# Six of sixteen units by ScalarE and TensorE, a new order of the units, and softplus right behind the silu

## The chip, the cores and the metric

The kernel runs on one core of one Trainium2 chip. Time is device time in microseconds (us) of one execution; the kernel before has a median of 26257.85 us over three runs (26257.84 to 26273.53).

## The reference, cut to what matters

Layer 0 is a two-dimensional Mamba block on x of shape (8, 64, 128, 128), along rows and along columns, forwards and backwards; layer 1 is a residual block of two 3x3 convolutions with batch norms. Nearly all of the time is in layer 0:

```python
def selective_scan(u, delta, A, Bm, Cm, D):
    def step(h, inp):
        u_t, d_t, B_t, C_t = inp
        dA = jnp.exp(d_t[..., None] * A)
        h = dA * h + (d_t * u_t)[..., None] * B_t[:, None, :]
        y = jnp.einsum('bdn,bn->bd', h, C_t)
        return (h, y)
    ...
    return jnp.transpose(ys, (1, 0, 2)) + u * D

def mamba(seq, p):                       # seq: sequences of 128 steps, 64 channels
    xz = jnp.einsum('blc,ec->ble', seq, in_w)
    x, z = (xz[..., :di], xz[..., di:])  # di = 128
    x = silu(causal_conv(x, conv_w, conv_b))
    xdbl = jnp.einsum('bld,ed->ble', x, xp_w)
    dt, Bm, Cm = ...                     # 4, 16 and 16 of xdbl
    delta = jax.nn.softplus(jnp.einsum('blr,dr->bld', dt, dt_w) + dt_b)
    A = -jnp.exp(A_log)                  # (128, 16)
    y = selective_scan(x, delta, A, Bm, Cm, Dp)
    y = y * silu(z)
    return jnp.einsum('bld,cd->blc', y, out_w)
```

The results of both directions and both orientations are averaged, group-normalized, passed through a silu and added to x.

## The kernel before, in words

**Groups.** The first stage, some 25,100 of the 26,239 us, is a loop over 512 groups: 8 images, 2 orientations (`o` 0 rows, 1 columns), 32 groups of four sequences each (N = 512 time steps side by side). A group computes both directions d. Its preparation (`prepare`) runs interleaved with the scans of the group before it.

**Units.** A group's state has 128 channels x 16 states x 2 directions. It is cut into 16 units: half (0 or 1: 64 channels), `ng` (four of the 16 states), d. A unit's tile is 128 partitions (32 channels x 4 states) by 1024 (two blocks of channels x 512 steps). `ORDER` (line 34) gives for each place r of 0 to 15 its (ng, d) and its kind; half is r % 2. Of every unit a scan is made on VectorE (`scan`, lines 453 and 455): s = dA * s + (delta u B). Then GpSimd multiplies it with C (`weigh`, line 460), and TensorE adds the states up in PSUM (`add_up`, line 476).

**Where the scan's two operands come from** depends on the kind:
- The decay exp(delta A) is a pair of ScalarE activations (`decay`, line 421) on the replicated `dl`. For V and G it goes to PSUM (`dA0`, `dA1`, one buffer per half, so that of unit r + 2 can only be written when scan r is done); for T into the unit's own tile `s` in SBUF, some steps early (`EARLY`).
- delta u B is for V a VectorE product of the replicated `du` with B rows that TensorE makes in PSUM (`drive` and `b_rows`, lines 430 and 410); for G the same product on GpSimd with B loaded by DMA (`b_tile`, line 403); for T sixteen ScalarE activations per ng (`spread`, line 372: X = duT times a column of BT) which both halves share, and eight TensorE transposes per unit (`turn`, line 439) into that half's PSUM buffer.

**The round trip.** `delta` and `delta u` come out of `prepare` with channels on partitions and have to be replicated over the four states. They are stored to DRAM (`keep`: `dd`, line 314, eight stores) and loaded back with each row repeated four times (`replicate`: `dl` and `du`, line 381, 512 KB each, four of each per group, five buffers each). B and C go the same way (`bd`, line 330, from `bc`, which ScalarE copies out of PSUM at line 328; `c` at line 395, 256 KB each, eight per group). All of these DMAs are issued by SP in the order of the program; an issue whose buffer is not free holds up those behind it.

**Order.** The order of instructions on every engine is written out by hand: under `tc.manual_schedule()` the loop at the end of the first stage goes through steps s, and in step r = s % 16 it emits, in this sequence: `b_rows` (table `ROWS`), `turn` or `decay` of unit r + 1, early decays (`EARLY`), the V drive of unit r + 1, G drives ahead of time (`AHEAD`), scan and weigh of unit r, the gate of the group before at r = 3 (`gate`, line 483), one piece of the next group's `prepare`, spreads (`SPREAD`), `add_up` four steps behind, and fetches of `c` and `bt` (`FETCH`). Every engine works its own list strictly in that order and waits where an operand or a buffer is not there.

`prepare` is a generator; each `yield` ends a step's piece. Before: step 1 z (`zp`), step 2 its copy to SBUF (line 285) and the convolution `cp` (line 290), step 5 silu of u (line 297) and of the z of the group before (line 299), step 6 the matmul `dp` (line 304), step 8 softplus (line 307), step 9 `bp`, the product delta u on VectorE (`du`, line 326), `bc`, `bd`, the decay of unit 11, `dl`, its two edge copies from `far` (line 336) and the stores. Steps 10 to 15 hold the replicating loads, transposes of `du` for T units, and BT (line 362).

Softplus, silu and exp need different activation tables on ScalarE; each change is an instruction ACT_TABLE_LOAD. Beside the groups run, for part of the time, the group norm of the image before (one silu and one addition per group) and its first convolution (one tile per group).

Of the kernel before, what the change touches and what calls it, by code (L numbers as in the profile page):

```python
# [9 lines left out]
F32 = mybir.dt.float32  # L10
# [36 lines left out]
def tile_mamba2d_then_resblock(ctx: ExitStack, tc: tile.TileContext, x, par, gn, p_w, o_w, new_p, bn, cst, out):  # L47
# [171 lines left out]
    with ExitStack() as st:  # L219
# [20 lines left out]
        far = big.tile([P, SEQ], F32, name="far")  # L240
# [33 lines left out]
        def prepare(g, before):  # L274
# [4 lines left out]
            zp = psa.tile([P, N], F32, name="zp", tag="b")  # L279
            nc.tensor.matmul(  # L280
                zp.rearrange("p (q t) -> p q t", t=W), w["wz"], g["xs"][0:C, :, PAD : PAD + W], start=True, stop=True
            )
            yield
            g["sz"] = work.tile([P, N], F32, name="sz", bufs=3)
            nc.scalar.copy(g["sz"], zp)
            cp = psm.tile([P, 2, N], F32, name="cp", tag="pt")
            for d in range(2):
# [6 lines left out]
                yield  # L294
            yield
            u = work.tile([P, 2, N], F32, name="u")
            nc.scalar.activation(u, cp, AF.Silu, bias=w["conv_b"])  # L297
            if before is not None:
                nc.scalar.activation(before["sz"], before["sz"], AF.Silu)
            g["u"] = u  # L300
            yield
# [3 lines left out]
            yield  # L305
            yield
            nc.scalar.activation(dp, dp, AF.Softplus, bias=w["dt_b"])
# [46 lines left out]
            bt = psm.tile([P, 2, N], F32, name="btp", tag="pt")[:, 0, 0 : 8 * SEQ]  # L354
            for q in range(SEQ):
                nc.tensor.matmul(
                    bt[:, 8 * q : 8 * (q + 1)], u[:, TD, W * q : W * (q + 1)], w["wbc"][:, 4 * TG : 4 * TG + 8],
                    start=True, stop=True,
                )
            yield  # L360
            g["BT"] = work.tile([P, 8 * SEQ], F32, name="BT", bufs=1)
# [5 lines left out]
        def spread(g, ng, q):  # L367

            t = g["X", ng, q] = work.tile([P, P, 4], F32, name="X", bufs=8)
            for n in range(4):  # L370
                k = 8 * q + 4 * (ng - TG) + n
                nc.scalar.activation(  # L372
                    t[:, :, n], g["duT"][:, q, :], AF.Copy, scale=g["BT"][:, k : k + 1]
                )
# [178 lines left out]
        def conv1(b):  # L553
# [49 lines left out]
        blocks, shared = {}, {}  # L603
# [12 lines left out]
        with tc.manual_schedule():  # L616
            stack(gs[0], 0)
            stack(gs[1], 1)
            for _ in prepare(gs[0], None):
                pass  # L620
            for r in (10, 11, 12, 14, 15):
# [7 lines left out]
            drive(*at(2))  # L629
            for s in range(total + UN):  # L630
# [5 lines left out]
                if r == 0:  # L636
                    for _ in pieces:
                        pass
                    pieces = prepare(after, this) if after else iter(())
# [3 lines left out]
                if r in ROWS and r != 9 and (g := after if r >= 14 else this):  # L643
# [3 lines left out]
                if kind != "T" and s + 1 < total and not (r == 10 and after):  # L647
# [12 lines left out]
                if s == total - 1:  # L660
                    nc.scalar.activation(this["sz"], this["sz"], AF.Silu)
# [12 lines left out]
                if r == 9 and live:  # L674
# [3 lines left out]
                if g := after if r >= 10 else this:  # L678
# [172 lines left out]
```

## Time and profile before

| | |
|---|---|
| median of three runs | 26257.85 us |
| span of the profiled execution, first to last instruction | 26239.0 us |
| VectorE (DVE), GpSimd (POOL) busy | 24018.6 and 24022.0 us, 92% each |
| ScalarE (ACT) busy | 22246.1 us, 85% |
| TensorE (PE) busy | 19212.0 us, 73% |
| DMA, mean share of 16 engines | 54.9% for the queue of SP |
| the 512 gates (line 483) | first at 185.7, last at 25124.0 us: 48.80 us per group |
| mean granted TensorE clock | 0.847 |

The profiled execution is one of its own; its span lies 18.9 us under the median, which has some time ahead of the first and behind the last instruction in it. In the lists of groups the columns are: line, engine, operation, output and inputs, count, then busy us and mean ns of one, then idle time of the engine before them and what ended it. A line of waits reads: who waited, for whom, us in total, times, longest. A line of the timeline reads: start, duration, engine, line, operation, and in brackets idle time before it and what ended that. A duration runs until the result is written; instructions of one engine overlap a little, so that the distance from start to start is shorter (a scan lasts 2.27 us, and the next starts 2.20 after it).

### The profile page before, as it was taken

The numbers are of one execution on the slowest core, as the hardware profiler recorded it, in microseconds if no ns is written. First come the engines' busy times: TensorE is split into PE (matmuls) and PEld (weight loads), VectorE is DVE, ScalarE is ACT, GpSimd is POOL, SyncE is SP. The second block draws the span as 40 slices with busy tenths as digits, with TensorE's granted clock in tenths as the row PEclk, the third lists the DMA queues.
The fourth block names the chain that finished last, engine by engine and source line by source line (L and its number), as shares of the span: only waits on it lengthen the run. The fifth ranks groups of instructions, "written<-read, shape, count | busy, mean of one in ns | idle before, by whom it ended". The sixth has DMA issues, their size and how long they took to land. (4 is left out here: it accounts for less than half of the span.)

```text
span 26239.0 us, 266043 instructions
## 1 busy us (share of the span) xinstructions
PE 19212.0 (73%) x75308; PEld 7191.5 (27%) x75308; DVE 24018.6 (92%) x14093; ACT 22246.1 (85%) x41390; POOL 24022.0 (92%) x10404
## 2 busy tenths in 40 slices
PE   6777777777777777777777777777777777777776
PEld 2222222222222223222232222222222222222232
DVE  8999999999999999999999999999999999999932
ACT  7888888888888888888888888888888888888842
POOL 7999999999999999999999999999999999999930
PEclk8888888888888888888888888888888888888888
DMA  5555555555555555555555555555555555555545
GB/s 166 173 175 171 176 186 174 178 169 174 190 171 177 169 177 189 170 176 169 184 182 175 172 176 183 177 177 171 175 185 175 175 171 177 186 172 175 172 140 190
DMA packets 2881499, 4604.73 MB, mean 175 GB/s; under 512 B 1055360, under 2 KB 1334032, under 8 KB 2864144
## 3 DMA queue, kind: packets, MB, share of 16 engines
q1 hardware_dynamic: 2859424, 4486.08, 54.9%
q10 hardware_dynamic: 15984, 68.06, 0.9%
q0 software_dynamic: 4608, 33.56, 0.3%
q8 instruction: 596, 9.76, 0.1%
q14 instruction: 887, 7.27, 0.1%
HBM read 3779.98 MB, written 738.98 MB: 172 GB/s over the span
## 5 line engine op out<-in xcount | busy, mean ns | idle before, releaser
L460 POOL TENSOR_TENSOR s<-s,c 128x1024 f32<-128x1024 f32 x8192 | 19201.7, 2372 | 983.2 <-issue 425.0
L421 ACT ACTIVATE dA<-dl,A 128x512 f32<-128x512 f32 x12288 | 8477.0, 690 | 2320.6 <-DVE s L455 1078.2
L455 DVE TENSOR_TENSOR_SCAN s<-dA,s 128x1024 f32<-128x1024 f32 x4096 | 9162.7, 2272 | 39.9 <-ACT dA L421 9.2
L430 DVE TENSOR_TENSOR s<-du,pb 128x1024 f32<-128x1024 f32 x4096 | 4930.2, 1204 | 1131.8 <-PE yp L476 556.0
L372 ACT ACTIVATE X<-duT,BT 128x128 f32<-128x128 f32 x16384 | 5603.1, 504 | 16.6
L430 POOL TENSOR_TENSOR s<-du,bt 128x1024 f32<-128x1024 f32 x2048 | 4841.3, 2364 | 154.7 <-DMA c<-bd 130.4
L410 PE MATMUL pb<-u,wb 128*128 128x512 f32 x4096 | 2776.4, 765 | 3009.8 <-ACT bc L328 2451.0
L476 PE MATMUL yp<-s,fold 128*32 128x512 f32 x32768 | 4932.0, 678 | 7.9 <-POOL s L460 7.7
L453 DVE TENSOR_TENSOR_SCAN s<-s,dA 128x1024 f32<-128x1024 f32 x2048 | 4666.1, 2278 | 52.9 <-PE dA L439 34.5
L453 DVE TENSOR_TENSOR_SCAN s<-dA,s 128x1024 f32<-128x1024 f32 x2048 | 4528.9, 2268 | 4.8 <-POOL s L430 4.1
L439 PE MATMUL dA<-ident,X 128*128 128x128 f32 x16384 | 2489.2, 301 | 783.3 <-DVE s L455 781.0
L290 PE MATMUL cp<-xs,wc 128*128 128x512 f32 x4096 | 2692.9, 792 | 140.5 <-ACT cs L572 139.7
L439 PEld LDWEIGHTS dA<-ident,X 128*128 128x128 f32 x16384 | 2034.7, 155 | 2597.1 <-DVE s L455 1892.9
L421 ACT ACTIVATE s<-dl,A 128x512 f32<-128x512 f32 x4096 | 2702.9, 707 | 0.0
L280 PE MATMUL zp<-xs,wz 64*128 64x512 f32 x1024 | 895.0, 968 | 1706.6 <-DVE s L430 1436.0
L410 PEld LDWEIGHTS pb<-u,wb 128*128 128x128 f32 x4096 | 715.2, 219 | 4487.4 <-ACT bc L328 2915.0
L476 PEld LDWEIGHTS yp<-s,fold 128*32 128x32 f32 x32768 | 824.0, 117 | 3298.8 <-issue 2282.6
L304 PE MATMUL dp<-u,wd 128*128 128x512 f32 x2048 | 1117.8, 672 | 332.7 <-ACT u L297 331.7
L421 ACT ACT_TABLE_LOAD x1030 | 1321.5, 1283 | 18.4
L290 PEld LDWEIGHTS cp<-xs,wc 128*128 128x128 f32 x4096 | 898.2, 243 | 1520.1 <-issue 969.0
L466 PE MATMUL yp<-u,dg 128*128 128x512 f32 x2048 | 961.2, 591 | 1.6 <-DVE y L483 1.6
L789 POOL DMA_DIRECT2D out<-cc x32 | 17.2, 538 | 971.9 <-ACT cc L788 971.9
(118 smaller groups left out, 13940.4 us busy)
## 6 DMA issues: line engine op xcount, KB each, us to landing
dl<-dd SPq DMA_DIRECT2D x2048, 512.0 KB
du<-dd SPq DMA_DIRECT2D x2048, 512.0 KB
c<-bd SPq DMA_DIRECT2D x4096, 256.0 KB
dd<-du SPq DMA_DIRECT2D x2048, 128.0 KB
dd<-dl SPq DMA_DIRECT2D x2048, 128.0 KB
bt<-bd SPq DMA_DIRECT2D x1024, 256.0 KB
xs<-x_h SPq DMA_DIRECT2D x512, 128.0 KB
bd<-bc SPq DMA_DIRECT2D x512, 128.0 KB
```

The lines of the kernel that those rows point to most:

```text
L290: nc.tensor.matmul(cp[:, d, :].rearrange("p (q t) -> p q t", t=W), w["wc"][:, d, k, :], g["xs"][:, :, t : t + W], start=k == 0, stop=k == 1,)
L304: nc.tensor.matmul(dp[:, d, :], w["wd"], u[:, d, :], start=True, stop=True)
L372: nc.scalar.activation(t[:, :, n], g["duT"][:, q, :], AF.Copy, scale=g["BT"][:, k : k + 1])
L410: nc.tensor.matmul(pb, wt[g["o"]]["wb"][:, P * ng : P * (ng + 1)], g["u"][:, d, :], start=True, stop=True)
L421: nc.scalar.activation(dA[:, j, :], g["dl", half, d][:, j, :], AF.Exp, scale=wt[g["o"]]["A"][:, 2 * half + j, ng : ng + 1])
L430: engine.tensor_mul(s, g["du", half, d], b.unsqueeze(1).to_broadcast([P, 2, N]))
L439: nc.tensor.transpose(dB[:, j, W * q : W * (q + 1)], g["X", ng, q][:, 32 * (2 * half + j) : 32 * (2 * half + j + 1), :].rearrange("p c n - ...
L453: nc.vector.tensor_tensor_scan(s, a, b, 0.0, ALU.mult, ALU.add)
L455: nc.vector.tensor_tensor_scan(s[:, ::-1], a[:, ::-1], b[:, ::-1], 0.0, ALU.mult, ALU.add)
L460: nc.gpsimd.tensor_mul(s, s, c.unsqueeze(1).to_broadcast([P, 2, N]))
L466: nc.tensor.matmul(g["yp"], wt[g["o"]]["dg"], g["u"][:, d, :], start=d == 0, stop=False, skip_group_check=True)
L476: nc.tensor.matmul(g["yp"][32 * q : 32 * (q + 1), :], fold, s[:, j, :], start=False, stop=r == UN - 2, skip_group_check=True,)
```

## The change

T units become six: both halves of ng 1, 2 and 3 in direction 0. G units become three, V units seven. Their order is new, and with it the tables. In `prepare`, z's matmul comes after the convolution, the copy of z is gone, silu of z is taken from PSUM in the same step as that of u; softplus follows one step later, without exps between; the two edge copies become one. `c` has six buffers instead of five. The fetches of `c12` and `c13` move from steps 6 and 8 to 9 and 11, and they stand in those steps behind the piece of `prepare`.

```diff
 ORDER = (
-    (0, 0, "V"), (0, 0, "V"), (1, 0, "G"), (1, 0, "G"), (2, 0, "T"), (0, 1, "V"), (0, 1, "V"), (2, 0, "T"),
-    (1, 1, "V"), (1, 1, "V"), (2, 1, "G"), (2, 1, "G"), (3, 0, "T"), (3, 1, "V"), (3, 1, "V"), (3, 0, "T"),
+    (0, 0, "V"), (0, 0, "V"), (1, 0, "T"), (2, 1, "G"), (0, 1, "V"), (0, 1, "V"), (2, 0, "T"), (1, 0, "T"),
+    (2, 1, "G"), (1, 1, "V"), (1, 1, "V"), (2, 0, "T"), (3, 0, "T"), (3, 1, "V"), (3, 1, "G"), (3, 0, "T"),
 )
-TG, TD = 2, 0
+TG, TD = 1, 0
+TN = 4 * (NG - TG)
...
-            zp = psa.tile([P, N], F32, name="zp", tag="b")
-            nc.tensor.matmul(
-                zp.rearrange("p (q t) -> p q t", t=W), w["wz"], g["xs"][0:C, :, PAD : PAD + W], start=True, stop=True
-            )
-            yield
-            g["sz"] = work.tile([P, N], F32, name="sz", bufs=3)
-            nc.scalar.copy(g["sz"], zp)
+            yield
             cp = psm.tile([P, 2, N], F32, name="cp", tag="pt")
...
+            zp = psa.tile([P, N], F32, name="zp", tag="b")
+            nc.tensor.matmul(
+                zp.rearrange("p (q t) -> p q t", t=W), w["wz"], g["xs"][0:C, :, PAD : PAD + W], start=True, stop=True
+            )
             yield
             u = work.tile([P, 2, N], F32, name="u")
             nc.scalar.activation(u, cp, AF.Silu, bias=w["conv_b"])
-            if before is not None:
-                nc.scalar.activation(before["sz"], before["sz"], AF.Silu)
+            g["sz"] = work.tile([P, N], F32, name="sz")
+            nc.scalar.activation(g["sz"], zp, AF.Silu)
             g["u"] = u
-            yield
             dp = psm.tile([P, 2, N], F32, name="dp", tag="pt")
             for d in range(2):
                 nc.tensor.matmul(dp[:, d, :], w["wd"], u[:, d, :], start=True, stop=True)
             yield
-            yield
             nc.scalar.activation(dp, dp, AF.Softplus, bias=w["dt_b"])
+            yield
+            yield
             yield
...
-            if before is not None:
-                decay(before, 11)
             dl = work.tile([P, 2, N], F32, name="dl", tag="nat")
             nc.scalar.copy(dl, dp)
-            for d, edge in enumerate((0, W - 1)):
-                nc.scalar.copy(dl[:, d, :].rearrange("p (s t) -> p s t", t=W)[:, :, edge], far)
+            edges = dl[:, :, 0:SEQ]
+            nc.scalar.copy(dataclasses.replace(edges, ap=[list(edges.ap[0]), [N + W - 1, 2], [W, SEQ]]), far)
...
-            g["BT"] = work.tile([P, 8 * SEQ], F32, name="BT", bufs=1)
+            g["BT"] = work.tile([P, TN * SEQ], F32, name="BT", bufs=1)
...
-            t = rep.tile([P, N], F32, name="c", bufs=5)
+            t = rep.tile([P, N], F32, name="c", bufs=6)
...
-        EARLY = {3: 4, 4: 7, 11: 12, 12: 15}
+        EARLY = {0: 2, 3: 6, 4: 7, 8: 11, 9: 12, 13: 15}
 
         SPREAD = {
-            14: [(2, 0)], 15: [(2, 1), (2, 2)], 0: [(2, 3)], 1: [(3, 0)], 2: [(3, 1)], 3: [(3, 2)], 4: [(3, 3)],
+            14: [(1, 0), (1, 1)], 15: [(1, 2)], 0: [(1, 3)], 1: [(2, 0)], 2: [(2, 1)], 3: [(2, 2)], 4: [(2, 3)],
+            7: [(3, 0), (3, 1)], 10: [(3, 2), (3, 3)],
         }
 
-        AHEAD = {15: 3, 0: 3, 7: 3, 8: 3}
+        AHEAD = {0: 3, 5: 3, 11: 3}
 
-        ROWS = {14: 0, 3: 5, 6: 8, 9: 13}
+        ROWS = {14: 0, 2: 4, 7: 9, 10: 13}
+        LATE = 10
 
         FETCH = {
-            10: ["c0", "b2"], 12: ["c2"], 14: ["c4"], 15: ["c5"], 2: ["c8"], 3: ["b10"], 4: ["c10"],
-            6: ["c12"], 8: ["c13"],
+            10: ["c0", "b3"], 12: ["c2"], 14: ["c3"], 1: ["c4"], 3: ["c6"], 5: ["c9"], 7: ["b14"],
+            9: ["c12"], 11: ["c13"],
         }
+        AFTER = (10, 12, 14)
...
-                if r == 9 and live:
+                if r == LATE and live:
                     b_rows(this, ROWS[r])
...
-                if g := after if r >= 10 else this:
+                if g := after if r in AFTER else this:
                     fetch(g, r)
```

More of the change, by code (lines that the diff above doesn't have):

```diff
@@ L1 @@
+import dataclasses
 from contextlib import ExitStack
@@ L239, in tile_mamba2d_then_resblock @@
             stacks.append(xs)
-        far = big.tile([P, SEQ], F32, name="far")
+        far = big.tile([P, 2, SEQ], F32, name="far")
         nc.vector.memset(far, FAR)
@@ L272, in stack, with prepare @@
                         nc.sync.dma_start(out=xs[es, :, t : t + HH], in_=g["xc"][hf * C : (hf + 1) * C])
-        def prepare(g, before):
+        def prepare(g):
             w = wt[g["o"]]
             yield
-            zp = psa.tile([P, N], F32, name="zp", tag="b")
-            nc.tensor.matmul(
-                zp.rearrange("p (q t) -> p q t", t=W), w["wz"], g["xs"][0:C, :, PAD : PAD + W], start=True, stop=True
-            )
             yield
-            g["sz"] = work.tile([P, N], F32, name="sz", bufs=3)
-            nc.scalar.copy(g["sz"], zp)
             cp = psm.tile([P, 2, N], F32, name="cp", tag="pt")
@@ L305, in prepare @@
             yield
+            nc.scalar.activation(dp, dp, AF.Softplus, bias=w["dt_b"])
             yield
-            nc.scalar.activation(dp, dp, AF.Softplus, bias=w["dt_b"])
+            yield
             yield
@@ L353, in prepare @@
             replicate(g, 1, 1)
-            bt = psm.tile([P, 2, N], F32, name="btp", tag="pt")[:, 0, 0 : 8 * SEQ]
+            bt = psm.tile([P, 2, N], F32, name="btp", tag="pt")[:, 0, 0 : TN * SEQ]
             for q in range(SEQ):
                 nc.tensor.matmul(
-                    bt[:, 8 * q : 8 * (q + 1)], u[:, TD, W * q : W * (q + 1)], w["wbc"][:, 4 * TG : 4 * TG + 8],
+                    bt[:, TN * q : TN * (q + 1)], u[:, TD, W * q : W * (q + 1)], w["wbc"][:, 4 * TG : 4 * TG + TN],
                     start=True, stop=True,
@@ L370, in spread @@
             for n in range(4):
-                k = 8 * q + 4 * (ng - TG) + n
+                k = TN * q + 4 * (ng - TG) + n
                 nc.scalar.activation(
@@ L618, in tile_mamba2d_then_resblock @@
             stack(gs[1], 1)
-            for _ in prepare(gs[0], None):
+            for _ in prepare(gs[0]):
                 pass
-            for r in (10, 11, 12, 14, 15):
+            for r in AFTER:
                 fetch(gs[0], r)
@@ L628, in tile_mamba2d_then_resblock @@
             drive(*at(0))
-            drive(*at(2))
+            if (r := UN - 1) in AHEAD:
+                drive(*at(AHEAD[r] - 1))
             for s in range(total + UN):
@@ L638, in tile_mamba2d_then_resblock @@
                         pass
-                    pieces = prepare(after, this) if after else iter(())
+                    pieces = prepare(after) if after else iter(())
                     if n + 2 < len(gs):
@@ L642, in tile_mamba2d_then_resblock @@
                 kind = ORDER[(r + 1) % UN][2]
-                if r in ROWS and r != 9 and (g := after if r >= 14 else this):
+                if r in ROWS and r != LATE and (g := after if r >= 14 else this):
                     b_rows(g, ROWS[r])
@@ L646, in tile_mamba2d_then_resblock @@
                     turn(*at(s + 1))
-                if kind != "T" and s + 1 < total and not (r == 10 and after):
+                if kind != "T" and s + 1 < total:
                     decay(*at(s + 1))
@@ L659, in tile_mamba2d_then_resblock @@
                     gate(prev)
-                if s == total - 1:
-                    nc.scalar.activation(this["sz"], this["sz"], AF.Silu)
                 if r == OUT and (prev or after):
```

## The prediction

> **What bounds the kernel now.** I read the page first (busy shares), then a window of a thousand us inside the long first stage, then the waits of VectorE, and then the timelines of the queues over two neighbouring groups. The page and the window:
>
> ```profile
> PE 19212.0 (73%) x75308; PEld 7191.5 (27%) x75308; DVE 24018.6 (92%) x14093; ACT 22246.1 (85%) x41390; POOL 24022.0 (92%) x10404
> L430 DVE TENSOR_TENSOR s<-du,pb 128x1024 f32<-128x1024 f32 x4096 | 4930.2, 1204 | 1131.8 <-PE yp L476 556.0
> 11315.00:12315.00 1000.00, 729.30 (x2922) 264.94 (x2921) 952.66 (x556) 888.13 (x1661) 958.24 (x412) 0.85 0.57 171
> ```
>
> VectorE and GpSimd are busy 95 to 96% of the first stage (third and fifth figure of the window), ScalarE 89%. So close to full, any of them could be the bound; the line of the V drives shows that VectorE idles mostly before one kind of instruction. Its waits:
>
> ```profile
> DVE s L430 <- PE yp L476: 556.0, 574, 3.8
> DVE s L430 <- DMA du<-dd: 528.5, 570, 14.3
> ```
>
> One wait per group is for `du`, the replicated tile that comes back from DRAM. VectorE's timeline over two groups (start, duration), and SP's over the same stretch:
>
> ```profile
> 11915.53 1.20 DVE L326 TENSOR_TENSOR du<-dp,u 128x1024 f32<-128x1024 f32 x1
> ...
> 11936.38 1.22 DVE L430 TENSOR_TENSOR s<-du,pb 128x1024 f32<-128x1024 f32 x1 [1.83 <-DMA du<-dd]
> ...
> 11964.47 1.20 DVE L326 TENSOR_TENSOR du<-dp,u 128x1024 f32<-128x1024 f32 x1
> ...
> 11985.64 1.22 DVE L430 TENSOR_TENSOR s<-du,pb 128x1024 f32<-128x1024 f32 x1 [1.13 <-DMA du<-dd]
> ```
>
> ```profile
> 11917.23 0.57 SPq L330 DMA_DIRECT2D bd<-bc  x1
> ...
> 11928.02 0.60 SPq L381 DMA_DIRECT2D du<-dd  x1
> ...
> 11966.17 0.56 SPq L330 DMA_DIRECT2D bd<-bc  x1
> ```
>
> The drive that waits is that of unit 1 of the next group. It closes a ring, and the ring is the period: drive 1 at 11936.38 to the `du` product at 11964.47 is 28.09 us of VectorE without a gap; 1.70 later SP issues `bd`; 19.47 after that the next drive 1 starts. The sum, 49.26, is exactly 11985.64 less 11936.38. Over all 512 groups the trace's times of DMA semaphores say the same: `du` of half 1 has landed 18.64 us after the issue of `bd` in the mean (90% between 17.7 and 19.9), and drive 1 starts 0.12 after the landing in the median group. So 28.1 + 1.6 + 18.76 = 48.5 against 48.80 measured from the 512 gates. VectorE's and GpSimd's idle time is what the ring leaves over; neither is the bound by itself. Within 18.76 no engine works for the ring: eight stores to DRAM, then replicating loads of 512 KB each, `du` of half 1 the sixth in SP's order.
>
> **The change, part by part.** ScalarE's rows, from its timeline some twelve groups earlier (start, duration), and the matmul that it will wait for:
>
> ```profile
> 11317.69 1.32 ACT L421 ACTIVATE s<-dl,A 128x512 f32<-128x512 f32 x2
> 11318.92 1.39 ACT L372 ACTIVATE X<-duT,BT 128x128 f32<-128x128 f32 x4
> 11320.10 1.41 ACT L421 ACTIVATE dA<-dl,A 128x512 f32<-128x512 f32 x2
> 11321.53 1.28 ACT L297 ACT_TABLE_LOAD   x1
> 11322.82 1.11 ACT L297 ACTIVATE u<-cp,conv_b 128x1024 f32<-128x1024 f32 x1
> 11323.84 0.62 ACT L299 ACTIVATE sz<-sz 128x512 f32<-128x512 f32 x1
> 11324.47 1.28 ACT L421 ACT_TABLE_LOAD   x1
> ...
> 11330.37 1.09 ACT L307 ACTIVATE dp<-dp,dt_b 128x1024 f32<-128x1024 f32 x1
> ```
>
> ```profile
> 11323.99 1.98 PE L304 MATMUL dp<-u,wd 128*128 128x512 f32 x4 [0.72 <-ACT u L297]
> ```
>
> From start to start: a pair of exps into PSUM 1.35 us (1.42 when a table load follows, which waits for its end), a pair into SBUF 1.21, four X 1.19, a table load 1.30.
>
> *Work per engine.* One V and one G unit become T. VectorE loses a drive (1.12 start to start), GpSimd one (2.36). TensorE gains 16 transposes, two times 1.05, at 73% busy. ScalarE gains 16 X (4.75) and loses: the copy of z (0.47), one `far` copy (0.10), one of four table loads (1.28), and 0.28 because two pairs of exps now go to SBUF; BT's 48 columns for 32 cost 0.02 at most. Net +2.6, from 43.2 busy (888.13 over 1000 us, times 48.6) to 45.8. By shares alone that would still fit into 48.
>
> *Where it lies in the ring.* VectorE's stretch from drive 1 to the `du` product holds four further drives before (5, 6, 8, 9) and four after (4, 5, 9, 10), ten scans and the gate in both. The drive that is saved lies behind the `du` product, under the DMA round trip. It is worth nothing.
>
> *ScalarE takes VectorE's place in the ring.* `bd` needs `bc`, and `bc` now stands behind everything that ScalarE does in steps 2 to 9. Let drive 1 start at 0. Drive 1.12, scan 0 2.20, scan 1 2.27, and 0.04 later, at 5.63, the exps of unit 3 may overwrite its PSUM. From there ScalarE has no gap of its own: exp 3 1.35, X 1.19, exp 4 1.35, exp 6 1.21, X 1.19, exp 5 1.35, exp 7 1.21, X 1.42, table 1.30, silu u 1.11, wait for `dp` 2.05, table 1.30, softplus 1.12, table 1.30, exp 8 1.35, eight X 2.36, exp 9 1.35, exp 11 1.21, exp 10 1.35, exp 12 1.21, `bc` and the issue 0.60: 27.88, so `bd` goes out at 33.51. Before, it went out at 28.1 + 1.6 = 29.7. The earlier gates of that chain are met (exp 4 may start 2.20 after exp 3 and is reached after 2.54).
>
> *Softplus behind the silu.* The one new wait. Before, six us of exps lay between silu and softplus and covered `dp`. Now the wait stands ahead of softplus' table load in ScalarE's queue (the built program has it there), and only the silu of z, 0.6, lies beside 2.05. Bounds: if the load slipped ahead of the wait, 1.30 less; the slowest twentieth of the groups has `dp` 3.45 after silu, 1.4 more. I take 2.05, the median row. Queued behind: exp 8, so scan 8; and on TensorE, whose `dp` stands between the transposes of units 6 and 7, scan 7 (some 1.4 late, inside scan 8's delay).
>
> *SP's queue.* `c12` and `c13` were fetched in steps 6 and 8, ahead of `bd`; now in 9 and 11, so `c12` goes between the stores and the first replicating load and `c13` right behind `du` of half 1. `c12` is issued where SP waits some 1.3 us for the stores anyway; its 256 KB cost the ring 0 to 0.7 (half of the 1.4 by which landings of 512 KB follow each other); I take 0. `c13` makes GpSimd wait: weigh 13 cannot start before 0.7 after drive 1. Then weighs 13, 14, 15 and the drive of unit 3, four by 2.34, end at 10.0; VectorE wants scan 3 at 8.8. It slips by 1.2, exp 5 waits for scan 3's end, and of that 0.44 is left in ScalarE's chain. Bounds 0 and 1.2; I take 0.44. The loads behind (`dl`, `du` of the other direction) move back by one `c`, 0.7, and the new order needs the last of them sooner: drive 4 reads its `du` 7.7 after drive 1, 26.5 after `bd`, and its landing moves from 25.8 to 26.5 in the mean by the semaphore times (28.2 in the slowest twentieth). Up to 1.2 of lateness lies inside scan 3's wait; I take nothing, the bound is 0.5. `z` after the convolution on TensorE, six `c` buffers, the late b row: covered by idle TensorE, nothing.
>
> *The sum.* 33.51 + 0.44 + 18.76 = 52.7 us a group, against 48.5 by the same working: +4.2, by 511 groups = 2,146 us. The profiled execution's span is 26,239.0; the median of the runs, 26,257.85, is 18.9 above it. Loading, the last convolution and the output stay. 26,258 + 2,146 = 28,400.
>
> By the Trainium skill (Perfetto Trace Analysis, Identifying the Most-Contended Engine) the engine of the highest occupancy is to be relieved first. Those are VectorE and GpSimd, and by that rule the change takes 1.12 us off each group and ends near 25,690; the row of drive 1's wait says that neither of them sets the period, so I don't go by it.
>
> The skill's ScalarE: Activation LUTs, What ACT_TABLE_LOAD costs, puts a switch of tables at 2.66 us with the drain. By it the load that is dropped would save twice what the rows show (1.28, and some 0.2 of drain), and the chain's three switches would be dearer by as much each; the trace decides.
>
> **Rivals.**
> - *Not slower: ScalarE keeps up.* If the chain from exp 3 to `bd` took 23.9 instead of 27.9, VectorE would again set `bd`, directly at the end of the `du` product: 28.1 + 1.2 + 18.76 = 48.1, or 26,050 (0.4 a group). For it: ScalarE's busy time of 45.8 fits. Against: exps into PSUM can't run ahead of the scans, so idle time in steps 12 to 1 doesn't help steps 2 to 9. It decides at 4.0 us off the chain.
> - *A shorter chain.* The table load and the scan 3 wait hidden: 52.7 - 1.3 - 0.4 = 51.0, or 27,530.
> - *GpSimd as the bound.* `c12` costs its 0.7, and `c13` lands later so that the whole 1.2 of scan 3 and some more stay: 54.2, or 29,170. For it: the two fetches sit in the densest stretch of transfers.
> - *That the change doesn't do what it says* is out for the table load: the built program has three per group for four.
>
> **How the numbers follow.** My forecast 0.74 (own range 27,850 to 28,900), shorter chain 0.09, GpSimd 0.07, ScalarE keeps up 0.10. The range, 27,450 to 29,000, takes in the shorter chain and leaves out the last two. Within 0.2% (52 us; about what this measurement can tell) is 0.03 of the last case, faster 0.07, slower 0.90.
>
> **What would show it.** A gate every 52 to 53 us; VectorE near 86%, GpSimd near 84%; SP's `bd` 33 to 35 us after drive 1; a wait of ScalarE for `dp` of some 1.4 us per group, 700 to 800 us in all; GpSimd waiting for `c` for thousands of us; drives 0 and 1 waiting for `du` longer than now. Wrong, if drive 1 no longer starts at `du`'s landing, or if `bd` comes 30 us after drive 1.

## The result, and the profile after

The changed kernel takes 29,095.6 us (29,069.1 to 29,133.1 over four runs), the kernel before 26,257.9: 1.108 times as long, with a 95% interval of 1.106 to 1.109. That is 2,838 us more, in the direction of the forecast of 28,400, and 96 us above the range's upper end of 29,000. The mean granted TensorE clock is 0.833, for 0.847 before; it does not explain the time, as a run below with 0.824 takes 725 us less.

The page of the changed kernel; the lines are those of GpSimd's weigh, TensorE's `add_up`, VectorE's V drives and softplus' table load (busy us, mean ns | idle before, and what ended most of it):

```profile
PE 21225.1 (73%) x83500; PEld 8628.1 (30%) x83500; DVE 23684.2 (81%) x13581; ACT 23825.3 (82%) x48046; POOL 22824.7 (78%) x9892
...
L458 POOL TENSOR_TENSOR s<-s,c 128x1024 f32<-128x1024 f32 x8192 | 19165.5, 2369 | 5039.9 <-DMA c<-bd 4539.9
...
L474 PE MATMUL yp<-s,fold 128*32 128x512 f32 x32768 | 6176.1, 691 | 3532.1 <-POOL s L458 3532.0
...
L428 DVE TENSOR_TENSOR s<-du,pb 128x1024 f32<-128x1024 f32 x3584 | 4332.2, 1209 | 2193.8 <-PE pb L408 1136.6
...
L305 ACT ACT_TABLE_LOAD x512 | 656.9, 1283 | 943.2 <-PE dp L303 943.2
```

The same thousand us as before (VectorE third, ScalarE fourth, GpSimd fifth figure):

```profile
11315.00:12315.00 1000.00, 733.56 (x2934) 298.55 (x2934) 831.93 (x467) 834.54 (x1692) 810.85 (x351) 0.84 0.52 159
```

VectorE, ScalarE and GpSimd all have more idle time than before, ScalarE too, which got the work: they are busy 83%, 83% and 81%, where they had 95%, 89% and 96%. TensorE stays at 73%. None of the four is full, so a chain of waits sets the time. The waits (total us, times, longest):

```profile
POOL s L458 <- DMA c<-bd: 4539.9, 974, 9.7
...
PE yp L474 <- POOL s L458: 3532.0, 936, 9.9
...
DVE s L428 <- DMA du<-dd: 1019.2, 911, 14.1
...
ACT L305 <- PE dp L303: 943.2, 512, 5.1
```

One round of the chain in the timelines of VectorE, GpSimd, TensorE, ScalarE and SP, in order of time:

```profile
13005.50 1.22 DVE L428 TENSOR_TENSOR s<-du,pb 128x1024 f32<-128x1024 f32 x1 [0.47 <-DMA du<-dd]
...
13006.26 7.00 POOL L458 TENSOR_TENSOR s<-s,c 128x1024 f32<-128x1024 f32 x3 [7.20 <-DMA c<-bd]
...
13008.67 1.92 PE L474 MATMUL yp<-s,fold 128*32 128x512 f32 x4 [7.82 <-POOL s L458]
...
13010.52 1.97 PE L437 MATMUL dA<-ident,X 128*128 128x128 f32 x8
...
13012.59 2.29 DVE L451 TENSOR_TENSOR_SCAN s<-s,dA 128x1024 f32<-128x1024 f32 x1 [1.49 <-ACT dA L419]
...
13014.92 1.42 ACT L419 ACTIVATE dA<-dl,A 128x512 f32<-128x512 f32 x2 [1.03 <-DVE s L451]
...
13027.20 1.28 ACT L305 ACT_TABLE_LOAD   x1 [1.63 <-PE dp L303]
...
13038.26 1.20 DVE L326 TENSOR_TENSOR du<-dp,u 128x1024 f32<-128x1024 f32 x1
...
13039.75 0.56 ACT L328 COPY bc<-bp 64x512 f32<-64x512 f32 x1
...
13040.34 0.57 SPq L330 DMA_DIRECT2D bd<-bc  x1
...
13046.67 0.55 SPq L393 DMA_DIRECT2D c<-bd  x1
...
13059.55 1.22 DVE L428 TENSOR_TENSOR s<-du,pb 128x1024 f32<-128x1024 f32 x1 [1.18 <-DMA du<-dd]
```

Drive 1 at 13005.50 to `bd` at 13040.34 is 34.84 us; the next drive 1 starts 19.21 later, again when `du` lands. Ahead of `bd` comes `bc` on ScalarE; the `du` product on VectorE had ended before it. So the ring now closes through ScalarE. Two more things are to be seen. `c` of unit 13 lands after drive 1; GpSimd's weigh 13 waits for it, TensorE's `add_up` waits for weigh 13, and the transposes that scan 2 reads stand behind that `add_up`. Scan 2 is 1.49 us late, and ScalarE's exps of unit 4, which overwrite scan 2's PSUM, 1.03. (The line of scan 2 names ScalarE's exp as the one that ended its wait: that exp, of unit 3, ended at 12.56, when the transposes ended too; it is the transposes that scan 2 reads.) And `c12`, at 13046.67, stands in SP's queue ahead of the replicating loads. (VectorE's 1,136.6 us of waiting for pb, the B rows that TensorE makes, are those of the drive of unit 13, which comes behind the `du` product and so lies beside the round trip.)

The pieces of the ring, each the mean over 502 groups of the trace, from start to start; landings by the times of the DMA semaphores. The rows below "changed" are runs of the next section:

| us per group | period | drive 1 to silu u | silu u to end of `bc` | drive 1 to `bd` | `bd` to landing of `du`, half 1 | landing to drive 1 |
|---|---|---|---|---|---|---|
| before | 48.83 | 18.01 | 11.93 | 29.96 | 18.64 | 0.23 |
| changed | 54.38 | 18.28 | 16.71 | 35.02 | 19.23 | 0.13 |
| c early | 52.98 | 17.25 | 16.76 | 34.05 | 18.79 | 0.15 |
| `du` first | 53.82 | 17.93 | 17.08 | 35.04 | 18.17 | 0.62 |
| X later | 51.35 | 17.45 | 14.88 | 32.35 | 18.77 | 0.22 |
| preparation up | 50.88 | 17.72 | 6.45 | 24.20 | 18.80 | 7.88 |
| before, `du` first | 48.63 | 18.00 | 12.14 | 30.32 | 17.54 | 0.77 |
| before, preparation up | 48.04 | 18.05 | 10.16 | 28.51 | 17.93 | 1.60 |
| before, new silu | 52.28 | 17.54 | 15.35 | 32.91 | 19.05 | 0.31 |

Of the 5.55 us that a group got longer, 5.06 lie between drive 1 and `bd`, and 0.59 between `bd` and the landing; drive 1 follows the landing 0.10 sooner.

### The profile page after: what moved, and what is told of

Same layout as the page of the kernel before. It is cut to its first block, busy times and chain, and to the rows that moved or that the text cites. A ratio compares the mean times of both kernels' runs of the same rounds, so it can differ in the third digit from the quotient of the medians.

```text
span 29088.8 us, 289749 instructions
## 1 busy us (share of the span) xinstructions
PE 21225.1 (73%) x83500; PEld 8628.1 (30%) x83500; DVE 23684.2 (81%) x13581; ACT 23825.3 (82%) x48046; POOL 22824.7 (78%) x9892
## 5 line engine op out<-in xcount | busy, mean ns | idle before, releaser
L453 DVE TENSOR_TENSOR_SCAN s<-dA,s 128x1024 f32<-128x1024 f32 x4096 | 9271.7, 2279 | 656.4 <-ACT dA L419 601.5
L474 PE MATMUL yp<-s,fold 128*32 128x512 f32 x32768 | 6176.1, 691 | 3532.1 <-POOL s L458 3532.0
L419 ACT ACTIVATE dA<-dl,A 128x512 f32<-128x512 f32 x10240 | 7070.1, 690 | 1731.5 <-DVE s L451 1503.2
L451 DVE TENSOR_TENSOR_SCAN s<-s,dA 128x1024 f32<-128x1024 f32 x3072 | 7004.4, 2280 | 1548.1 <-PE dA L437 1115.1
L370 ACT ACTIVATE X<-duT,BT 128x128 f32<-128x128 f32 x24576 | 8148.1, 502 | 16.6
L428 DVE TENSOR_TENSOR s<-du,pb 128x1024 f32<-128x1024 f32 x3584 | 4332.2, 1209 | 2193.8 <-PE pb L408 1136.6
L437 PE MATMUL dA<-ident,X 128*128 128x128 f32 x24576 | 4274.9, 331 | 745.8 <-DVE s L453 725.1
L437 PEld LDWEIGHTS dA<-ident,X 128*128 128x128 f32 x24576 | 3592.6, 173 | 3780.4 <-issue 1951.6
L419 ACT ACTIVATE s<-dl,A 128x512 f32<-128x512 f32 x6144 | 4068.4, 710 | 9.7
L428 POOL TENSOR_TENSOR s<-du,bt 128x1024 f32<-128x1024 f32 x1536 | 3632.8, 2365 | 130.9 <-PE pb L408 130.7
L451 DVE TENSOR_TENSOR_SCAN s<-dA,s 128x1024 f32<-128x1024 f32 x1024 | 2285.7, 2274 | 0.0
L321 PE MATMUL bp<-u,xpT 128*32 128x512 f32 x2048 | 816.2, 888 | 1600.5 <-DVE s L428 1600.5
```

The costliest lines, as they stand in the source:

```text
L321: nc.tensor.matmul(bp[2 * NS * d : 2 * NS * (d + 1), :], w["wbc"], u[:, d, :], start=True, stop=True, skip_group_check=True,)
L370: nc.scalar.activation(t[:, :, n], g["duT"][:, q, :], AF.Copy, scale=g["BT"][:, k : k + 1])
L419: nc.scalar.activation(dA[:, j, :], g["dl", half, d][:, j, :], AF.Exp, scale=wt[g["o"]]["A"][:, 2 * half + j, ng : ng + 1])
L428: engine.tensor_mul(s, g["du", half, d], b.unsqueeze(1).to_broadcast([P, 2, N]))
L437: nc.tensor.transpose(dB[:, j, W * q : W * (q + 1)], g["X", ng, q][:, 32 * (2 * half + j) : 32 * (2 * half + j + 1), :].rearrange("p c n - ...
L451: nc.vector.tensor_tensor_scan(s, a, b, 0.0, ALU.mult, ALU.add)
```

## The experiments

The kernel before, measured again beside these runs, took 26,268 to 26,312 us, where it took 26,257.9 beside the result. So a difference between runs from different occasions is good to some 50 us, or 0.1 us a group. Ratios are to the kernel before as measured beside the run.

**The two fetches.** The changed kernel, with `c` of units 12 and 13 fetched where the kernel before fetches them.

```diff
-            9: ["c12"], 11: ["c13"],
+            6: ["c12"], 8: ["c13"],
```

> The changed kernel with the fetches of c12 and c13 back in steps 6 and 8, ahead of bd in SP's queue; nothing else. Theory (GpSimd's late weigh 13 holds up TensorE's add_up of units 12 and 13, behind which the transposes of unit 2 stand, and with it scan 2, exp 4 and the whole chain of ScalarE; and c12 delays the round trip): GpSimd's wait for c, 4540 us in all, goes; silu u starts 17.2 us after drive 1 instead of 18.3; du of half 1 lands 18.6 after bd instead of 19.2. 1.1 + 0.6 = 1.7 us a group, so 29096 - 870 = 28230 us. Rival (GpSimd's wait lies wholly beside the round trip, only the chain and the round trip as forecast set the period): at most the 0.6 of the round trip, 28790 us or more.

Measured: 28,370.6 us, 1.078 times before (1.0765 to 1.0797). That is 725 us less, 1.42 a group; the theory's figure was 28,230. GpSimd's wait for `c` is gone from its waits, whose first lines now are:

```profile
POOL s L458 <- DVE s L451: 1268.4, 904, 6.2
POOL out L789 <- ACT cc L788: 980.9, 32, 753.5
```

and VectorE's scan 2 follows scan 1 directly:

```profile
13046.22 1.22 DVE L428 TENSOR_TENSOR s<-du,pb 128x1024 f32<-128x1024 f32 x1 [0.46 <-DMA du<-dd]
13047.36 4.46 DVE L451 TENSOR_TENSOR_SCAN s<-dA,s 128x1024 f32<-128x1024 f32 x2
13051.77 2.29 DVE L451 TENSOR_TENSOR_SCAN s<-s,dA 128x1024 f32<-128x1024 f32 x1
```

By the table 1.03 us came back between drive 1 and silu, and 0.44 between `bd` and the landing. So the two late fetches are a quarter of the loss; the rest, 2,113 us, is something else. The run moves both at once and does not part `c12`'s share from `c13`'s.

**Softplus behind other exps.** The changed kernel, with softplus one step later, so that `dp` is covered, at the price of a fourth table load.

```diff
-            nc.scalar.activation(dp, dp, AF.Softplus, bias=w["dt_b"])
             yield
+            nc.scalar.activation(dp, dp, AF.Softplus, bias=w["dt_b"])
             yield
```

> The changed kernel with softplus one step later, behind the exps of unit 8, as an exp stood between silu and softplus before: four table loads a group instead of three, dp covered. Theory (bc stands behind the whole of ScalarE's list, so what counts is its length: the 1.6 us of waiting go, a load of 1.3 and its drain come): the period stays within 0.4 us; a little is won in the groups with a convolution, where dp comes later. 28900 to 29150 us. Rival (scan 8 waits for softplus, and that lateness is the price): scan 8 can start some 4 us sooner, so the 1.6 of the wait come back: 28280 us.

Measured: 29,374.2 us (1.1144 to 1.1177 of before), 279 more than the changed kernel and above the theory's band too; the rival falls. The wait for `dp`, 1.84 us a group, is gone, one more load came in (1.28), and ScalarE's exps now wait longer for scans:

```profile
ACT dA L419 <- DVE s L451: 1924.5, 1959, 4.3
```

against 1,503.2 in the changed kernel, 0.82 a group more. From silu to `bc` 0.49 us are added. So softplus right behind the silu costs no more here than covering its wait does. (The Trainium skill, ScalarE: Activation LUTs, What ACT_TABLE_LOAD costs, has 2.66 us for a switch with its drain. An estimate from the three parts, 1.84 less, one switch and 0.82 more, gives 1.6 with that figure and 0.26 with the row's 1.28; measured are 0.49, so the row is nearer here.)

**`du` ahead of c0 and b.** In both kernels the 256 KB loads c0 and b of the first G unit are issued behind `du` of half 1 instead of ahead of it. The changed kernel, and then the kernel before:

```diff
-            10: ["c0", "b3"], 12: ["c2"], 14: ["c3"], 1: ["c4"], 3: ["c6"], 5: ["c9"], 7: ["b14"],
+            12: ["c0", "b3", "c2"], 14: ["c3"], 1: ["c4"], 3: ["c6"], 5: ["c9"], 7: ["b14"],
...
-            10: ["c0", "b2"], 12: ["c2"], 14: ["c4"], 15: ["c5"], 2: ["c8"], 3: ["b10"], 4: ["c10"],
+            11: ["c0", "b2"], 12: ["c2"], 14: ["c4"], 15: ["c5"], 2: ["c8"], 3: ["b10"], 4: ["c10"],
```

> The changed kernel with c0 and b3 fetched two steps later, so that du of half 1 is the fourth replicating load and not the sixth; no byte less, no instruction of another engine moved. Theory (drive 1 waits for du's landing and closes the ring): du of half 1 lands 1.4 us sooner after bd; du of half 0, which is not moved, leaves drive 1 free some 0.8 sooner, so between 0.8 and 1.4 us a group: 28400 to 28700 us. Rival (the engines' own work sets the period; transfers are hidden): no change, 29096 us, or slower, as c0 and b3 come later.

> The kernel before with c0 and b2 fetched one step later, behind du of half 1: the same single move as in the changed kernel. Theory (the same ring sets the kernel before: drive 1, du product, bd, du's landing): 0.8 to 1.2 us a group, 25650 to 25850 us, unless GpSimd, 96% busy, takes over at 47.5 us a group (25600). Rival (VectorE and GpSimd, each 92% busy, are the bound): no change, 26258 us, or slower because c0 and b2 come later.

Measured: 28,809.0 us for the changed kernel (1.0931 to 1.0968) and 26,152.2 for the one before (0.9924 to 0.9954). Both get faster, so the round trip is in both rings; both get less than the theory's figure. The landing came 1.06 and 1.10 us sooner, as wanted, but only part of it reached the period, 0.56 and 0.20 (each good to some 0.1): drive 1 now starts 0.6 to 0.8 after the landing, since `du` of half 0, which drive 0 waits for, did not come sooner. In the kernel before GpSimd now waits for its B too:

```profile
POOL s L430 <- DMA bt<-bd: 653.2, 388, 3.9
```

**ScalarE's list.** On top of the early fetches, eight X are made after `bc` instead of ahead of it: same work, another order.

```diff
-            7: [(3, 0), (3, 1)], 10: [(3, 2), (3, 3)],
+            10: [(3, 0), (3, 1), (3, 2), (3, 3)],
```

> The edit, on top of the run with c of units 12 and 13 fetched early (28,370.6 us, 52.98 us a group): the eight exps' arguments X of units (3,0) and (3,1), which ScalarE makes in step 7 ahead of the copy bc of B, are made in step 10 instead. ScalarE does the same work; only what stands ahead of bc in its queue is shorter, by about 2.3 us (8 small copies). Theory (the ring of the du round trip is closed by ScalarE's list between drive 1 and bc): bd is issued earlier by as much, the group falls from 52.98 to about 50.7 us, and the time to about 27,200 us (27,000 to 27,500, since the du product's end on VectorE may bind before all 2.3 us are won). Rival (ScalarE's total work, or VectorE's, sets the period, and the order within the list is of no matter): unchanged, 28,370 within 100.

Measured: 27,547.5 us (1.0468 to 1.0503), 823 less, 1.61 a group for 2.36 of list. It falls 50 us short of the theory's band, and the rival, no change, is out. The list from silu to `bc` became 1.88 shorter; by then the `du` product on VectorE, which starts 31.86 after drive 1 and takes 1.2, ends later than `bc`.

**The whole end of the preparation, one to three steps earlier.** Again on top of the early fetches. Softplus stays in step 6; the B projection, `bc` and `bd` move from step 9 to 6, the `du` product and the stores from 9 to 7, the loads of half 0 from 10 to 8 and those of half 1 from 11 to 10.

```diff
             nc.scalar.activation(dp, dp, AF.Softplus, bias=w["dt_b"])
+            bp = psa.tile([P, N], F32, name="bp", tag="b")
...
+            nc.scalar.copy(bc, bp[0 : 4 * NS, :])
...
+            nc.sync.dma_start(out=bd.rearrange("n d t -> d n t"), in_=bc)
...
+            nc.scalar.copy(dl, dp)
...
             yield
+            nc.vector.tensor_mul(du, dp, u)
+            keep(0, dl)
+            keep(1, du)
             yield
+            replicate(g, 0, 0)
             yield
-            bp = psa.tile([P, N], F32, name="bp", tag="b")
...
-            keep(1, du)
-            keep(0, dl)
             yield
...
                 nc.tensor.transpose(dt[:, c], du[:, TD, c], ident)
-            replicate(g, 0, 0)
+            replicate(g, 1, 0)
             yield
...
             nc.scalar.copy(g["duT"].rearrange("p q c -> p (q c)"), dt)
-            replicate(g, 1, 0)
...
-            7: [(3, 0), (3, 1)], 10: [(3, 2), (3, 3)],
+            8: [(3, 0)], 9: [(3, 1)], 10: [(3, 2), (3, 3)],
```

> The edit, on top of the same run (28,370.6 us): the end of the preparation is moved up. Softplus, the B projection, its copy bc and the store bd stand one step earlier (step 6), the du product and its stores in step 7, and the replication loads of half 0 and half 1 in steps 8 and 10; X of (3,0) and (3,1) move to steps 8 and 9. No work is added or taken away. Theory (the ring through du is what sets 52.98 us, and not the load on the engines): du ends some 26 us after drive 1, the round trip comes to about 44 us and leaves the ring, and the next bound is the busiest engine, ScalarE at 45.8 us a group and VectorE at 45.2, with a few us of waits: 47 to 49 us a group, 25,300 to 26,300 us. Rival (the engines' waits on each other, softplus ahead of the exps of later units above all, cost as much as the ring): above 27,500 us.

Measured: 27,303.5 us (1.0376 to 1.0407). `bd` goes out 24.2 us after drive 1, and `du` lands 7.88 us before drive 1 needs it: the round trip has left the ring, by far. And yet the period is 50.9, not 47 to 49. The theory had the ring right and the next bound wrong; the rival's figure is missed as well, though what it said is nearer. VectorE's waits, and the window:

```profile
DVE s L450 <- PE dA L436: 1219.7, 1364, 4.1
DVE s L427 <- PE pb L407: 755.5, 512, 2.6
...
DVE s L452 <- ACT dA L418: 342.8, 501, 1.1
DVE du L331 <- ACT dl L317: 338.9, 512, 17.3
```

```profile
11315.00:12315.00 1000.00, 707.71 (x3101) 308.89 (x3099) 894.38 (x507) 897.55 (x1838) 871.30 (x374) 0.84 0.53 168
```

VectorE and ScalarE are both at 89 to 90%, and the four waits shown, 5.2 us a group, are for TensorE and ScalarE, not for a DMA. Which of them sets the 50.9 stays open.

**A like move, one step, in the kernel before.**

```diff
                 nc.tensor.matmul(dp[:, d, :], w["wd"], u[:, d, :], start=True, stop=True)
             yield
-            yield
             nc.scalar.activation(dp, dp, AF.Softplus, bias=w["dt_b"])
...
-            if before is not None:
-                decay(before, 11)
...
             keep(0, dl)
             yield
+            if before is not None:
+                decay(before, 11)
+            replicate(g, 0, 0)
+            yield
...
                 nc.tensor.transpose(dt[:, c], du[:, TD, c], ident)
-            replicate(g, 0, 0)
+            replicate(g, 1, 0)
             yield
...
             nc.scalar.copy(g["duT"].rearrange("p q c -> p (q c)"), dt)
-            replicate(g, 1, 0)
```

> The edit, on the kernel before: softplus one step earlier (7 instead of 8), and with it the B projection, the du product, bc, bd and the stores of du and dl (step 8 instead of 9); the loads of half 0 in step 9 and of half 1 in step 10 ahead of c0 and b2, which come behind them. Units, their engines and all instructions are the same. Theory (the round trip of du sets the period before as well): the du product comes one scan and one drive, 2.3 to 3.4 us, earlier after drive 1, and the du of half 1 lands 1.1 us sooner after bd, as the run that moved c0 and b2 showed; the ring falls from 48.8 to about 45 us and leaves the bound to VectorE's own work, 24,019 us or 46.9 us a group: 47.0 to 47.8 us a group, 25,350 to 25,750 us. It is then also what the changed kernel with the same move (27,303 us, 50.9 us a group) is to be set against: two units' products moved from VectorE and GpSimd to ScalarE and TensorE would cost some 1,600 to 1,950 us even where the round trip binds neither. Rival (another wait closes right behind it, as in the run with c0 and b2 moved alone, which won 0.12 ms instead of the 0.4 to 0.6 expected): 26,000 us or more.

Measured: 25,858.8 us, 0.9847 of before (0.9831 to 0.9864), between theory and rival, 109 above the theory's band. It is faster than both kernels. Drive 1 starts 1.6 us after the landing, so the ring is off the path here too:

```profile
11315.00:12315.00 1000.00, 722.23 (x2972) 270.70 (x2972) 966.72 (x566) 898.46 (x1696) 973.94 (x419) 0.91 0.58 176
```

VectorE and GpSimd are both busy 97% (third and fifth figure); which of the two now sets the pace, the run does not say. The granted TensorE clock is higher as well, 0.882 for 0.847; what part of the gain is due to that was not tested. Set against the 27,303.5 us of the run above: where the round trip binds neither, the changed kernel's arrangement is 1,445 us slower than the old one, 2.8 us a group.

**One half of the change alone.** The kernel before with the new silu and softplus, its units left as they were (z's matmul to step 4, silu of z from PSUM, `dp` in step 5, softplus in step 6).

```diff
-            zp = psa.tile([P, N], F32, name="zp", tag="b")
...
-            nc.scalar.copy(g["sz"], zp)
...
+            zp = psa.tile([P, N], F32, name="zp", tag="b")
...
+            nc.scalar.activation(g["sz"], zp, AF.Silu)
             g["u"] = u
-            yield
             dp = psm.tile([P, 2, N], F32, name="dp", tag="pt")
...
             yield
-            yield
             nc.scalar.activation(dp, dp, AF.Softplus, bias=w["dt_b"])
+            yield
+            yield
             yield
```

> One part of the change alone, on the kernel before: the gate's z is projected in step 4 and its silu read from PSUM, right behind the silu of u, and softplus follows one step behind them (step 6 instead of 8), with TensorE's dp in step 5; the four units on ScalarE and TensorE, the order of the units, and the step of the du product stay as before. ScalarE's work falls by one table load and one copy a group (1.28 + 0.58 us), and it waits for dp some 1.6 us in their place. Theory (the loss comes with the two more units, which put ScalarE's list in VectorE's place between drive 1 and bd): the ring still goes through VectorE's 28.1 us, so the time stays within 150 us of the kernel before, 26,110 to 26,410. Rival (the wait for dp ahead of softplus is what costs, as ScalarE's exps behind it come late for VectorE): 1.6 to 4.2 us a group, 27,000 us or more.

Measured: 28,003.7 us (1.0652 to 1.0683). The theory is out by 1,600 us; the rival's figure holds. VectorE, whose largest waits were 556 and 529 us, now waits 4.5 us a group for pb, the B rows of unit 8:

```profile
DVE s L428 <- PE pb L408: 2292.8, 503, 6.3
```

That is not quite the rival's reason, which had the exps come late. Two of the edits could do it: `dp`, which stands ahead of pb on TensorE and waits for the silu, or z, which sits in the one PSUM buffer that pb needs. Two runs part them. The first puts `dp` and softplus behind what unit 8 needs:

```diff
             g["u"] = u
+            yield
             dp = psm.tile([P, 2, N], F32, name="dp", tag="pt")
...
             nc.scalar.activation(dp, dp, AF.Softplus, bias=w["dt_b"])
             yield
             yield
-            yield
```

> The edit, on the run with the new silu and softplus alone (28,003.7 us): TensorE's dp in step 6, behind pb of unit 8, instead of step 5 ahead of it, and softplus in step 7, behind the exps of unit 8, instead of step 6 ahead of them. The z of the gate is still projected in step 4 and its silu read from PSUM. In the run before, VectorE waited 4.6 us a group for pb of unit 8, which stood behind dp on TensorE, while dp waited for the silu. Theory (dp and softplus ahead of what unit 8 needs cost the 3.4 us a group): most of the 1,734 us comes back; what may stay is the wait of pb of unit 8 for the PSUM buffer that z holds until its silu has read it, some 1.3 us a group by the places of both in the trace of the kernel before (silu of z would end 0.1 us after drive 8 starts, and pb takes 1.1), so 26,150 to 26,950 us. Rival (z in PSUM is what costs): 27,400 us or more.

The second puts z in PSUM alone into the kernel before with its preparation moved up, whose `dp` and softplus stand behind pb:

```diff
-            zp = psa.tile([P, N], F32, name="zp", tag="b")
...
-            nc.scalar.copy(g["sz"], zp)
...
+            zp = psa.tile([P, N], F32, name="zp", tag="b")
...
+            nc.scalar.activation(g["sz"], zp, AF.Silu)
```

> The edit, on the kernel before with its preparation moved up (25,858.8 us): the z of the gate is projected in step 4 instead of 1 and its silu read from PSUM right behind the silu of u, without the copy to SBUF; dp and softplus stay in steps 6 and 7. The one part of the change that takes work off ScalarE (0.58 us a group), alone. Theory (ScalarE isn't the bound here, and z holds its PSUM buffer past the point where pb of unit 8 wants it): 0 to 1.3 us a group more, 25,850 to 26,500 us. Rival (ScalarE's shorter list counts): faster by the 0.58 us, 25,560 us or less.

Measured: 27,463.1 us (1.044 to 1.0471) and 27,384.4 us (1.0409 to 1.0444). The first is where the rival put it: moving `dp` back returns only 541 of the 1,746 us. The second is outside both bands: z in PSUM alone costs 1,526 us, 3.0 a group. So z is the larger part, where both theories had it as the smaller. VectorE still waits for pb in the last run, 3.8 us a group:

```profile
DVE s L428 <- PE pb L408: 1953.4, 507, 4.6
```

and its timeline shows from where, TensorE's and VectorE's lines together:

```profile
13042.42 1.19 DVE L428 TENSOR_TENSOR s<-du,pb 128x1024 f32<-128x1024 f32 x1
...
13043.76 2.04 PE L290 MATMUL zp<-xs,wz 64*128 64x512 f32 x2 [2.67 <-DVE s L428]
...
13045.73 3.78 PE L464 MATMUL yp<-u,dg 128*128 128x512 f32 x4
...
13049.44 1.52 PE L474 MATMUL yp<-s,fold 128*32 128x512 f32 x8
...
13050.89 1.13 PE L408 MATMUL pb<-u,wb 128*128 128x512 f32 x2
```

z has to wait until VectorE's drive of unit 6 has read the B rows of units 5 and 6 out of the buffer that they share. TensorE stands still for 2.67 us, and `skip`, `add_up` and pb of unit 8 come behind, while VectorE has only two scans, 4.46 us, until it wants pb. TensorE's waits for this buffer ahead of z, in this run and in the one that it builds on, with z in step 1:

```profile
PE zp L290 <- DVE s L428: 1749.1, 511, 4.9
```

```profile
PE zp L280 <- DVE s L430: 821.5, 321, 4.6
```

So the buffer was often taken in step 1 too. But there VectorE, behind the drive of unit 1 that z waits for, has four scans and the gate ahead of the drive of unit 5, the next that needs pb, and loses nothing. The expectation counted only how long z holds the buffer, 1.3 us, and neither TensorE's wait ahead of z nor what it does between z and pb.

**The other half alone.** In the changed kernel z goes by way of SBUF again, as before; and then `dp` and softplus go back too, which leaves the six units and their order.

```diff
             yield
+            zp = psa.tile([P, N], F32, name="zp", tag="b")
...
             yield
+            g["sz"] = work.tile([P, N], F32, name="sz", bufs=3)
+            nc.scalar.copy(g["sz"], zp)
...
-            nc.scalar.activation(g["sz"], zp, AF.Silu)
+            nc.scalar.activation(g["sz"], g["sz"], AF.Silu)
```

> One part of the change undone, on the changed kernel (29,095.6 us): the z of the gate is projected in step 1 again and copied from PSUM to SBUF by ScalarE in step 2; its silu stands behind the silu of u as in the changed kernel. Softplus, the six units and the order stay. Theory (in the changed kernel z in PSUM costs nothing: its trace shows TensorE at dp 0.06 us after the silu of u ends, and pb of unit 9 well ahead of its drive): the copy comes on top in ScalarE's list, 0 to 0.6 us a group, 29,096 to 29,400 us. Rival (z holds back TensorE here too, as in the run with z in PSUM on the kernel before, where it cost 3.0 us a group): 2 us a group less or more, 28,100 us or less.

> The other half of the change alone: six units on ScalarE and TensorE in the new order, with the silu of z by way of SBUF, TensorE's dp in step 6 and softplus in step 8 as in the kernel before. It is the run before (z by way of SBUF) with dp and softplus moved back too. Theory (the two parts press on one list of ScalarE, so that their costs don't add: softplus behind the silu saves two table loads, and costs the wait for dp, about as much): no better than the changed kernel, 29,100 to 29,800 us. Rival (the parts add up: 26,258 before, and the new silu and softplus alone cost 1,734 us of the 2,838): about 27,350 us, 27,700 or less.

Measured: 29,611.5 us (1.1244 to 1.1281) and 29,553.4 us (1.1225 to 1.1259). In the first the copy costs 1.0 us a group, more than its 0.58: ScalarE waits for z's matmul, which here stands behind the blocked `add_up`:

```profile
ACT sz L287 <- PE zp L282: 682.5, 469, 58.5
```

That is 212 above the first theory's band, and far from its rival, as z back in SBUF wins nothing here. In the second the theory's figure holds, and its rival falls: the parts don't add up. That one list of ScalarE is the reason is not shown by this.

| us | old silu and softplus | new silu and softplus |
|---|---|---|
| four units, old order | 26,258 | 28,004 |
| six units, new order | 29,553 | 29,096 |

The six units with their order cost 3,296 us alone; the two late fetches are in both figures of that row. The new silu and softplus cost 1,746 in the old order, and in the new order they win 458. With 516 of it lost when z goes back by way of SBUF, where its matmul stands behind the `add_up` that the late fetches hold up, the 458 may be smaller with early fetches; that was not run.

## Why the prediction was right and where it was wrong

*The ring, and ScalarE in VectorE's place.* Right. Drive 1 still starts when `du` lands, and `bd` waits for ScalarE. Shown by the runs: less list ahead of `bc` with the same work (X later) brought the time down by 823 us, an earlier landing by 287, and neither takes any work away.

*The price of ScalarE's chain, 33.51 us from drive 1 to `bd`.* Nearly right. With the late fetches out of the way it measures 34.05. The 0.5 lie between silu and `bc`: the median group of the changed kernel takes 16.34 us there, as the sum had it (16.3), the 112 groups that also carry a convolution 17.9 in the mean; there ScalarE waits 2.78 for `dp`, in the others 1.58. I had priced all groups by the median row of `dp`, 2.05.

*"I take 0.44": the wait that `c13` causes.* This step failed. I led it from GpSimd's late weigh 13 over the drive of unit 3 to scan 3, and let exp 5 lose 0.44. In the trace exp 5 waits for nothing; it goes another way, over TensorE's `add_up` of units 12 and 13, whose place ahead of the transposes of unit 2 I had not looked up, to scan 2 and exp 4. Undone by the early fetches it gave 1.03 us a group.

*"Its 256 KB cost the ring 0 to 0.7; I take 0."* Mis-sized within its bounds: the landing came 0.59 later than before, and 0.44 of it went with the two fetches. Both terms together are 1.42 us a group, 725 us, where 0.44 or 225 us had been set; the 500 us between are most of the 696 by which the forecast fell short. The groups with a convolution, which bring the mean between silu and `bc` 0.4 us above the sum's 16.3, make about the rest.

*The rival "GpSimd as the bound", 29,170 us at a chance of 0.07.* It named these two fetches as the cause and came nearest to the time; its chance was too small, and cutting it out set the range's upper end at 29,000. GpSimd itself is no bound: it idles 19%.

*Softplus behind the silu, 2.05 us.* Nearly right: of the 2.05, 1.4 were to be waiting, 700 to 800 us in all; 1.84 and 943 were measured. What I did not see is that the alternative costs as much in this order: covered, it was 279 us slower.

*"z after the convolution on TensorE ... covered by idle TensorE, nothing."* Right in the changed order, where undoing it cost 516 us, but not for that reason: TensorE is as idle in the old order, and there it cost 3.0 us a group. In the changed kernel's trace the next drive that needs pb behind z, that of unit 9, comes 10.3 us after it, where in the old order VectorE had only two scans, 4.46 us:

```profile
13020.05 1.09 PE L292 MATMUL zp<-xs,wz 64*128 64x512 f32 x2 [0.94 <-DVE s L428]
...
13030.31 1.20 DVE L428 TENSOR_TENSOR s<-du,pb 128x1024 f32<-128x1024 f32 x1
```

*The rival "ScalarE keeps up", 26,050 us.* Its point was 4.0 us off the chain. The run with the preparation moved up took 10.8 off and got no further than 27,303: past the ring the period stays at 50.9 us, with VectorE waiting for TensorE and ScalarE, and does not come down to VectorE's own stretch at 48.1.

*The marks.* `bd` 33 to 35 us after drive 1: 35.0. Gates every 52 to 53 us: 54.4. VectorE and GpSimd 86% and 84% of the stage: 83% and 81%, as the longer period makes them. GpSimd waiting for `c`: 4,540 us. Drives waiting longer for `du`: 1,019 us for 529. The skill's page Perfetto Trace Analysis (Identifying the Most-Contended Engine) would have the engine of the highest occupancy optimized first. The prediction's estimate by that rule was 25,690; the change relieves the two busiest engines, and the kernel got 2,838 us slower. In the run that took the round trip off the old kernel's path, where VectorE and GpSimd are at 97%, the rule may hold; no run relieved them there.

## What to carry to other kernels

Look for the ring first: when engines stand at 95% and one wait per period ends at a DMA's landing, add up the pieces of the round, and ask of a change what it puts ahead of the instruction that starts the transfer, in that engine's own list. When a transfer is moved back, follow its waiter through the in-order list of every engine behind it, to the third engine too; the wait comes out where something unrelated stands behind the one that waits. And once a ring is found, shorten it where it costs nothing: moving the same instructions one step earlier made the old kernel 1.5% faster.

## What the runs showed that was not expected

- One PSUM buffer shared by three short uses cost 3.0 us a group, 1,526 us, when one use moved by three steps, though ScalarE had one copy less to make.
- Two loads of 256 KB taken from ahead of another in one queue brought its landing forward by 1.06 and 1.10 us in the two kernels; only 0.56 and 0.20 of it reached the period, because a second landing lay right behind.
- Softplus' table load never ran ahead of the wait for its input: in all 512 groups it began only when the matmul was done, in the changed kernel after 1.84 us of idle time a group, in the kernel before with the new silu alone after 4.0.
